# A state-space convolution and an fp8 feed-forward network: sequences sorted by length, gate and up only over those that reach a chunk

## The chip, the cores and the metric

The kernel runs on one core of a Trainium2 chip. The metric is the device time of one execution in microseconds (us), taken as the median of several runs. The engines are TensorE (PE in the profile, its weight loads PEld), VectorE (DVE), ScalarE (ACT), GpSimd (POOL) and SyncE (SP), which issues DMAs. Every engine works through its own instructions in order and waits for the others by semaphores.

## The reference

There are 128 sequences (B) of 32 channels, called heads here (H), and 512 positions (L). Each head is convolved causally with a kernel of its own that a state-space model gives (64 complex modes), plus a skip term D; positions at or past the length of their sequence are set to zero. The result goes through a gated feed-forward network with fp8 rounding before each product, and x is added. Lengths are drawn from 78 to 453.

```python
y = causal_conv(x, K) + x * D[:, None]            # K: 32 heads x 512 taps, from log_dt, C, A
y = y * (arange(512)[None, :] < length[:, None])[:, None, :]
g = fp8(y) @ gate_w.T                             # gate_w, up_w: 1376 x 512
u = fp8(y) @ up_w.T
hidden = silu(g * sg) * (u * su)
out = x + fp8(hidden) @ down_w.T * sd             # down_w: 512 x 1376
```

## The kernel before

Positions lie on the partitions, in four chunks of 128 (LC). The 32 heads are taken in eight groups of four (HG); the columns of a group are its four heads by 128 sequences, T = 512 columns. The weights stay in SBUF from the start, as bf16 views of the f32 that was loaded (every second bf16). The hidden size 1376 is taken in eleven chunks of 128 (IC).

At the start the kernel builds a table of the taps in three batches of heads (`Powers`: 4, 12 and 16 heads), writes it to DRAM, and reads it back as Toeplitz blocks (`toeplitz`, tile `st`). Meanwhile `keep_busy` issues matmuls on zeros (tile `still`). The tables of the later batches are made between other work; those of the last batch on VectorE behind the residual adds of groups 0 and 1 (`between`).

A convolution (`convolve` for heads 0 to 15, `convolve8` for 16 to 31) multiplies f32 Toeplitz blocks, the stationary operand, with chunks of x. It uses sums of chunks (`xs`), which an accumulating DMA from GpSimd makes (L111 to L121), and ends in two PSUM tiles, `sp` and `cp`. ScalarE copies `sp` out; VectorE adds it to `cp` and writes fp8 `q` (L566), then sets the masked positions to zero (L576). Two ScalarE sums over `q` at the end of a group look for values that aren't finite (L580).

`gate_up` makes, for each of the eleven chunks, a gate and an up accumulation of four matmuls each (L612: weights stationary, `q` moving, 512 columns). ScalarE applies silu (L620), VectorE multiplies (L621). `quantise` rounds the product to fp8 in batches of one or two chunks: one ScalarE instruction (L594) and three VectorE instructions (L597 to L599). `Down` multiplies the result `hq` with the down weights (L654: weights stationary, `hq` moving) in four units, one for each chunk of positions; `put_out` adds x (L667), and SP stores the unit.

The stages of two groups are interleaved: after the last gate and up matmul of group g, TensorE runs convolutions of group g + 1 and the down units of g in turn. The order within an engine comes from a scheduler that follows the program order and the readiness of operands, except where `with after(...)` sets an instruction behind another on the same engine. PSUM holds eight tiles of 512 columns: two each of `gp` (also `sp`), `up`, `dp` and `cp`. A second, exact path (`wide`) runs behind a test at the end if a check has failed.

Of the kernel before, what the change touches and what calls it, by code (L numbers as in the profile page):

```python
# [9 lines left out]
F32 = mybir.dt.float32  # L10
# [47 lines left out]
def ssm_fp8_ffn(  # L58
    ctx: ExitStack,
    tc: tile.TileContext,  # L60
    xT: bass.AP,
    lens: bass.AP,
# [5 lines left out]
    outT: bass.AP,  # L68
# [13 lines left out]

    const = ctx.enter_context(tc.tile_pool(name="const", bufs=1))
# [7 lines left out]

    AT = [0, 2, 1, 3]


    SUMS = [(0, 1), (1, 2), (0, 2)]

    def chunk_of(g, c):
        return xT[AT[c] * P : (AT[c] + 1) * P, g * HG : (g + 1) * HG, :].rearrange("p h b -> p (h b)")

    def add_chunks(xg, n):  # L100
        xs = xp.tile([P, len(SUMS), T], F32, name="xs", bufs=1)
        for s, (c0, c1) in enumerate(SUMS[:n]):
            nc.vector.tensor_add(xs[:, s, :], xg[:, AT[c0], :], xg[:, AT[c1], :])
        return xs

    def load_sums(g, n):

        xs = xp.tile([P, len(SUMS), T], F32, name="xs", bufs=1)
        x0, x1, x2 = (chunk_of(g, c) for c in range(3))
        if n == 1:  # L110
            nc.gpsimd.dma_start(xs[:, 0, :], x1)  # L111
            nc.gpsimd.dma_start(xs[:, 0, :], x0, accum_op=ALU.add)
            return xs

        def twice(x):
            return x.unsqueeze(1).to_broadcast([P, 2, T])

        nc.gpsimd.dma_start(xs[:, 0:2, :], twice(x1))  # L118
        nc.gpsimd.dma_start(xs[:, 2, :], x0)
        nc.gpsimd.dma_start(xs[:, 0, :], x0, accum_op=ALU.add)  # L120
        nc.gpsimd.dma_start(xs[:, 1:3, :], twice(x2), accum_op=ALU.add)  # L121
        return xs

    def load_x(g):
        xg = xp.tile([P, LC, T], F32, name="xg")
        nc.sync.dma_start(
            xg.rearrange("p c (h b) -> p c h b", b=B),
            xT[:, g * HG : (g + 1) * HG, :].rearrange("(c p) h b -> p c h b", p=P),
        )
        return xg  # L130
# [3 lines left out]
    len_i = const.tile([P, B], I32, name="len_i")  # L134
    nc.sync.dma_start(len_i, lens.to_broadcast([P, B]))
# [30 lines left out]
    EIGHT = len(batches) - 1  # L166

    RB, RZ = 2 * P // NB, P // NB  # L170
    NRS = [(3 if n == EIGHT else 2) * RB + NA for n in range(len(batches))]
    KPS = [(NR + RZ) * NB for NR in NRS]
    kpads = [dram.tile([h1 - h0, KPS[n]], F32, name=f"kpad{n}") for n, (h0, h1) in enumerate(batches)]
    kts = [kg.tile([NRS[n] + RZ, h1 - h0, NB], F32, name=f"kt{n}") for n, (h0, h1) in enumerate(batches)]
# [22 lines left out]
    last = kg.tile([1, NRS[0]], F32, name="last")  # L197
    nc.gpsimd.memset(last, 0.0)
    nc.gpsimd.memset(last[:, NRS[0] - 1 :], 1.0)

    last8 = kg.tile([1, NRS[EIGHT]], F32, name="last8")

    gas = [kg.tile([P, w, NR + RZ], F32, name=f"ga{n}") for n, (w, NR) in enumerate(zip((HG, HB), NRS[::2]))]
# [41 lines left out]
    keep_busy(12)  # L245
    keep_busy(10, wim)

    class Powers:
# [67 lines left out]
        def products(self):  # L316
# [9 lines left out]
            NR = NRS[self.n]  # L326
# [8 lines left out]
            sums = pair(0, RB)  # L335
            yield nc.vector.tensor_sub(sums, pair(k0, RB), pair(k0 + RZ, 0))
            if self.n == EIGHT:
                yield nc.vector.tensor_sub(sums, sums, pair(k0 + 2 * RZ, RZ))
                yield nc.vector.scalar_tensor_tensor(
                    ga[:, :, 2 * RB : 3 * RB], ga[:, :, k0 + RB : NR], -1.0, ga[:, :, k0 + RB + RZ :], ALU.mult, ALU.subtract  # L340
                )

        def response(self, behind=None):
            NR = NRS[self.n]
# [3 lines left out]
            done = nc.tensor.matmul(kp[:, :, NB - 1], last8 if self.n == EIGHT else last, sm[0:1, 5, self.hs], start=False, stop=True)  # L348
# [48 lines left out]
    len_f = const.tile([P, B], F32, name="len_f")  # L397
    with after(coeffs_there):
        nc.gpsimd.tensor_copy(len_f, len_i)
        row_i = const.tile([P, LC], I32, name="row_i")  # L400
        nc.gpsimd.iota(row_i, pattern=[[P, LC]], base=P - 1, channel_multiplier=-1)
        row_f = const.tile([P, LC], F32, name="row_f")
        nc.gpsimd.tensor_copy(row_f, row_i)


    def build_mask(m, value, chunks=range(LC)):
        for c in chunks:
            done = nc.gpsimd.tensor_scalar(m[:, AT[c], :], len_f, row_f[:, c : c + 1], value, ALU.is_gt, ALU.mult)
        return done

    mask = const.tile([P, LC, B], U8, name="mask")
    all_bits = const.tile([P, 1], F32, name="all_bits")
    with after(first_done):
        nc.vector.memset(all_bits, 255.0)
    with after(copied):
        xs0 = add_chunks(x0, 1)
    with after(build_mask(mask, all_bits, range(1))):
        if IP > I:
            nc.gpsimd.memset(gw[:, :, I:], 0.0)
            nc.gpsimd.memset(uw[:, :, I:], 0.0)  # L420
            nc.gpsimd.memset(dw[I - FI * P :, FI, :], 0.0)
        done = build_mask(mask, all_bits, range(1, LC))
    with after(done):
        for kt in kts[1:]:
            nc.gpsimd.memset(kt, 0.0)
        nc.gpsimd.memset(gas[1][:, :, NRS[EIGHT] :], 0.0)
        nc.gpsimd.memset(last8, 0.0)
        NR = NRS[EIGHT]
        for row, d in ((2 * RB - RZ - 1, -1.0), (3 * RB - RZ - 1, -1.0), (NR - 1, 1.0)):
            nc.gpsimd.memset(last8[:, row : row + 1], d)  # L430
# [3 lines left out]

    shared = [const.tile([P, LC, B], F32, name=f"shared{n}") for n in range(HG)]
    with after(coeffs_there):
        for t in shared:
            nc.gpsimd.memset(t[:, 0, :], 0.0)
    chk = ctx.enter_context(tc.tile_pool(name="chk", bufs=1))

    def toeplitz(pool, h):

        n = next(n for n, (_, h1) in enumerate(batches) if h < h1)
        own = 3 if n == EIGHT else 2
        st = pool.tile([P, 6, P], F32, name="st")
        kpad, at = kpads[n], kpads[n].offset + (h - batches[n][0]) * KPS[n]
        done = nc.sync.dma_start(st[:, 3:6, :], bass.AP(kpad.tensor, at + (2 * own + 1) * P, [[1, P], [1, 3 * P]]))
        done = nc.sync.dma_start(st[:, 3 - own : 3, :], bass.AP(kpad.tensor, at, [[1, P], [2 * P, own], [1, P]]))
        return st, done

    def convolve8(st, xg, xs, j, scale, pool, before, bufs):

        b = slice(j * B, (j + 1) * B)
        k3, k2, k1, K2, K1, K0 = (st[:, n, :] for n in range(6))
        sp = ps.tile([P, 3, B], F32, name="sp", tag="gp")
        for n, k in enumerate((K2, K0, K1)):  # L460
            nc.tensor.matmul(sp[:, n, :], k, xs[:, n, b], start=True, stop=True)  # L461

        sh = pool.tile([P, 4, B], F32, name="sh", bufs=bufs)
        with after(before) if before else ExitStack():
            copied = nc.scalar.activation(sh[:, 0:3, :], sp, AF.Copy, scale=scale)  # L465
        with after(copied):
            copied = nc.scalar.activation(sh[:, 3, :], sp[:, 0, :], AF.Copy, scale=scale)
        t = shared[j]
        nc.vector.tensor_add(t[:, 1:4, :], sh[:, 0:3, :], sh[:, 1:4, :])
        cp = ps.tile([P, LC, B], F32, name="cp")  # L470
        nc.tensor.matmul(cp[:, 0:4:3, :], K0, xg[:, 0:4:3, b], start=True, stop=False)  # L471
        for c, k, x in ((3, k3, 0), (1, k1, 2), (2, k2, 1)):
            done = nc.tensor.matmul(cp[:, AT[c], :], k, xg[:, AT[x], b], start=c != 3, stop=True)  # L473
        return cp, pairs(t), done, copied

    def convolve(h, st, xg, xs, j, scale, pool, before=None, bufs=2):

        if h >= batches[EIGHT][0]:
            return convolve8(st, xg, xs, j, scale, pool, before, bufs)
        b = slice(j * B, (j + 1) * B)
        k3, k2, K2, K1, K0 = (st[:, n, :] for n in range(1, 6))
        sp = ps.tile([P, B], F32, name="sp", tag="gp")
        nc.tensor.matmul(sp, K2, xs[:, 0, b], start=True, stop=True)  # L487
        t = shared[j]
        with after(before) if before else ExitStack():
            copied = nc.scalar.activation(t[:, 1, :], sp, AF.Copy, scale=scale)  # L490
        cp = ps.tile([P, LC, B], F32, name="cp")
        nc.tensor.matmul(cp, K0, xg[:, :, b], start=True, stop=False)  # L492

        nc.tensor.matmul(cp[:, 2:4, :], K1, xg[:, 0:2, b], start=False, stop=False)  # L494
        nc.tensor.matmul(cp[:, 1, :], k2, xg[:, 2, b], start=False, stop=False)  # L495
        done = nc.tensor.matmul(cp[:, 3, :], k3, xg[:, 0, b], start=False, stop=True)  # L496
        return cp, twice(t[:, 0:2, :]), done, copied

    def pairs(y):

        return y.rearrange("p (k c) b -> p k c b", k=2)

    def twice(t):
        return t.unsqueeze(1).to_broadcast([P, 2, 2, B])
# [414 lines left out]
```

## Time and profile before

| | us |
|---|---|
| median of 3 runs (318.44 to 321.06) | 319.95 |
| the profiled execution | 318.58 |
| its span, first to last instruction | 316.8 |
| TensorE busy | 306.5 |
| VectorE busy | 265.4 |
| ScalarE busy | 182.5 |
| GpSimd busy | 29.6 |

The profiled execution is one run; its span runs from the first to the last instruction, and 1.78 us of its time lie around it. The lines that the prediction shows come from the profile's page and from queries of the same trace. A line of the groups has the program line, the engine, the operation, output and inputs, the shapes and the count; then the busy time in us and the mean ns of one; then the idle time of the engine just before these instructions and what ended it. A line of the windows has the stretch, its length, and the busy us of PE, PEld, DVE, ACT and POOL with their counts, the granted TensorE clock, the DMA share and GB/s. A line of the timeline or the chain begins with start and duration. A line of the waits says who waited for whom, how long in all, how often, and the longest. In the DMA lines the last figure is the median time from issue to landing.

### The profile page before, as it was taken

The numbers are of one execution on the slowest core, as the hardware profiler recorded it, in microseconds if no ns is written. First come the engines' busy times: TensorE is split into PE (matmuls) and PEld (weight loads), VectorE is DVE, ScalarE is ACT, GpSimd is POOL, SyncE is SP. The second block draws the span as 40 slices with busy tenths as digits, with TensorE's granted clock in tenths as the row PEclk, the third lists the DMA queues.
The fourth block names the chain that finished last, engine by engine and source line by source line (L and its number), as shares of the span: only waits on it lengthen the run. The fifth ranks groups of instructions, "written<-read, shape, count | busy, mean of one in ns | idle before, by whom it ended". The sixth has DMA issues, their size and how long they took to land.

```text
span 316.8 us, 4622 instructions
## 1 busy us (share of the span) xinstructions
PE 306.5 (97%) x1575; PEld 164.5 (52%) x1575; DVE 265.4 (84%) x477; ACT 182.5 (58%) x372; POOL 29.6 (9%) x72
## 2 busy tenths in 40 slices
PE   8899799999999999999999999999999999999992
PEld 2465346544555446644476446744476446744441
DVE  5985899789988899648998599958998599968992
ACT  5836568557683568446674477546664477266600
POOL 5621000010001000120001200120001200000000
PEclk9999999999999999999999999999999999999998
DMA  3599999562038500599036961389035830020004
GB/s 106 182 284 383 354 360 305 158 160 106 7 85 240 170 1 2 118 302 255 2 99 156 239 170 31 107 282 220 29 99 136 242 55 2 3 98 2 1 33 143
DMA packets 33922, 45.34 MB, mean 143 GB/s; under 512 B 3651, under 2 KB 20035, under 8 KB 33891
## 3 DMA queue, kind: packets, MB, share of 16 engines
q1 hardware_dynamic: 29603, 34.61, 34.8%
q0 software_dynamic: 3232, 7.87, 11.8%
q10 hardware_dynamic: 1056, 2.49, 2.1%
q8 instruction: 14, 0.23, 0.3%
q14 instruction: 17, 0.14, 0.1%
HBM read 36.41 MB, written 8.55 MB: 142 GB/s over the span
## 4 chain that ended last, share of the span: by engine, by line
PE 88%; DMA 5%; DVE 3%; ACT 1%; issue 1%; POOL 0%; DVEq 0%; POOLq 0%; ACTq 0%
PE dp L654 24%; PE up L612 22%; PE gp L612 22%; PE cp L492 4%; DMA uw<-upT 4%; PE sp L461 3%; PE cp L473 3%; PE cp L471 2%; PE cp L494 2%; PE sp L487 1%; PE cp L496 1%; PE cp L495 1%; DMA sm<-ssm 1%; PE kp L347 1%; ACT L208 0%
## 5 line engine op out<-in xcount | busy, mean ns | idle before, releaser
L612 PE MATMUL up<-q,uw 128*128 128x512 fp8e4 x352 | 90.3, 379 | 2.1 <-DMA uw<-upT 2.1
L612 PE MATMUL gp<-q,gw 128*128 128x512 fp8e4 x352 | 90.3, 379 | 0.2 <-DVE q L576 0.2
L620 ACT ACTIVATE s<-gp,psc 128x512 f32<-128x512 f32 x88 | 59.9, 682 | 51.0 <-PE gp L612 50.8
L654 PE MATMUL dp<-hq,dw 128*128 128x512 bf16 (+1 forms) x363 | 79.8, 373 | 0.0
L621 DVE SCALAR_TENSOR_TENSOR v<-up,psc,s 128x512 f32<-128x512 f32 x88 | 65.9, 748 | 14.8 <-PE up L612 11.7
L597 DVE SCALAR_TENSOR_TENSOR v<-m,v 128x1024 f32<-128x1024 bf16 (+1 forms) x56 | 55.8, 996 | 6.3 <-ACT m L594 5.4
L594 ACT ACTIVATE m<-v 128x1024 bf16<-128x1024 f32 (+1 forms) x56 | 48.8, 871 | 17.8 <-DVE v L621 17.3
L612 PEld LDWEIGHTS <-uw 128*128 128x128 bf16 x352 | 34.3, 98 | 44.2 <-DMA uw<-upT 3.0
L612 PEld LDWEIGHTS <-gw 128*128 128x128 bf16 x352 | 34.3, 98 | 41.6 <-DVE q L576 0.3
L598 DVE SCALAR_TENSOR_TENSOR hq<-m,v 128x1024 bf16<-128x1024 bf16 (+1 forms) x56 | 55.6, 993 | 0.1
L654 PEld LDWEIGHTS <-dw 128*128 128x128 bf16 x363 | 35.5, 98 | 36.0
L667 DVE SCALAR_TENSOR_TENSOR xg<-dp,nsc,xg 128x512 f32<-128x512 f32 (+1 forms) x33 | 24.0, 731 | 11.7 <-PE dp L654 11.4
L566 DVE SCALAR_TENSOR_TENSOR q<-cp,inv,shared 128x512 fp8e4<-128x512 f32 x32 | 23.9, 748 | 8.2 <-PE cp L496 8.2
L580 ACT ACTIVATE s<-q 128x1024 bf16<-128x1024 fp8e4 x16 | 16.8, 1048 | 18.3 <-DVE q L576 18.3
L599 DVE TENSOR_SCALAR hq<-hq 128x1024 bf16<-128x1024 bf16 (+1 forms) x56 | 20.6, 367 | 0.2
L465 ACT ACTIVATE sh<-sp,inv 128x384 f32<-128x384 f32 x16 | 9.2, 572 | 15.9 <-PE sp L461 15.9
L492 PE MATMUL cp<-xg,st 128*128 128x512 f32 x32 | 16.4, 594 | 0.0
L243 PE MATMUL nothing<-still 128*128 128x512 bf16 x48 | 13.5, 442 | 1.4 <-POOL still L180 1.4
L461 PEld LDWEIGHTS sp<-xs,st 128*128 128x128 f32 x96 | 12.9, 192 | 1.7
L473 PEld LDWEIGHTS cp<-xg,st 128*128 128x128 f32 x96 | 13.2, 191 | 0.8
L118 POOL DMA_DIRECT2D xs<-xT x4 | 3.0, 753 | 112.0 <-PE sp L461 79.1
L461 PE MATMUL sp<-xs,st 128*128 128x128 f32 x96 | 13.3, 275 | 0.0
(145 smaller groups left out, 241.4 us busy)
## 6 DMA issues: line engine op xcount, KB each, us to landing
st<-kpad SPq DMA_DIRECT2D x48, 192.0 KB, 4.1
xg<-xT SPq DMA_DIRECT2D x8, 1024.0 KB, 8.8
outT<-xg SPq DMA_DIRECT2D x31, 256.0 KB, 4.0
xs<-xT POOLq DMA_DIRECT2D x8, 512.0 KB, 7.9
xs<-xT POOLq DMA_DIRECT2D x14, 256.0 KB, 5.5
dw<-downT SPq DMA_DIRECT2D x1, 2560.0 KB, 13.8
st<-kpad SPq DMA_DIRECT2D x16, 128.0 KB, 4.8
gw<-gateT SPq DMA_DIRECT2D x2, 768.0 KB, 8.9
```

The costliest lines, as they stand in the source:

```text
L461: nc.tensor.matmul(sp[:, n, :], k, xs[:, n, b], start=True, stop=True)
L473: done = nc.tensor.matmul(cp[:, AT[c], :], k, xg[:, AT[x], b], start=c != 3, stop=True)
L492: nc.tensor.matmul(cp, K0, xg[:, :, b], start=True, stop=False)
L566: nc.vector.scalar_tensor_tensor(pairs(q[:, :, j * B : (j + 1) * B]), pairs(cp), inv[:, 0:1], t, ALU.mult, ALU.add, saturate=False,)
L594: done = nc.scalar.activation(m[:, 0:F], v, AF.Abs, scale=2.0**20 * (1.0 + 2.0**-6), accum_out=acc)
L597: nc.vector.scalar_tensor_tensor(v, m[:, 0:F], 1.5 * 2.0**14, v, ALU.max, ALU.add)
L598: nc.vector.scalar_tensor_tensor(out, m[:, 0:F], 1.5 * 2.0**14, v, ALU.max, ALU.subtract)
L612: multiplied = nc.tensor.matmul(o, w[:, c, i * P : (i + 1) * P], q[:, AT[c], :], start=(c == 0), stop=(c == LC - 1),)
L620: nc.scalar.activation(s, gp, AF.Silu, scale=pgate)
L621: product = nc.vector.scalar_tensor_tensor(v[:, (i - i0) * T : (i - i0 + 1) * T], up, pup, s, ALU.mult, ALU.mult)
L654: done = nc.tensor.matmul(self.dps[n], dm[:, i, c * P : (c + 1) * P], self.hq[:, i, t0:t1], start=(i == 0), stop=(i == IC - 1),)
L667: added = nc.vector.scalar_tensor_tensor(o, self.dps[n], ndown, o, ALU.mult, ALU.add)
```

## The change

The sequences are ranked by length on the chip: VectorE counts for each sequence how many are longer (a key of length and number keeps the order strict), and a 128 x 128 permutation in bf16 is made from the ranks. The convolution now has x as the stationary operand and the Toeplitz blocks as the moving one, so `q` comes out with sequences on the partitions. `sort` multiplies each chunk of `q` of a head with the first columns of the permutation, 128, 124, 84 and 40 of them (`CAPS`) for the four chunks; this transposes and sorts at once, and ScalarE copies the result to `qs` in fp8. Gate and up then stream only these columns for each chunk. If more sequences reach a chunk than it has columns, `fits` sends the kernel to the wide path.

All heads use one convolution of 1152 columns; `convolve8`, its further sums and its longer tables are gone. In the down product `hq` is the stationary operand and the weights are the moving one; a unit is now a head, with sequences on the partitions in sorted order. The x that is added is gathered by an indirect DMA from GpSimd (`load_sorted`, 1 MB a group), and the output is scattered by one indirect DMA for each unit, also from GpSimd, instead of a store from SP. The x for the convolution has one buffer instead of three.

The order is written out anew. `gate_up` chains matmuls and VectorE instructions; `STEPS` says how many VectorE steps of the quantise jobs follow each product, nine in all (jobs 0 to 2). The other four jobs come later: job 3 ahead of the first convolution output, job 4 ahead of the third, jobs 5 and 6 behind the fourth. The down units start behind all four convolutions. The checks of `q` come behind the sixth silu of `gate_up`. All loads of gate and up weights are issued from SP. `keep_busy` has two matmuls more at each of two places.

```diff
+    CAPS = [B, 124, 84, 40]
+    OFF = [sum(CAPS[:c]) for c in range(LC)]
+    NQ = sum(CAPS)
+
+    CHUNKS = [3, 1, 2, 0]
...
+    def load_sums(g):
+
+        xs = xp.tile([P, T], F32, name="xs", bufs=1)
+        nc.gpsimd.dma_start(xs, chunk_of(g, 1))
+        return xs, nc.gpsimd.dma_start(xs, chunk_of(g, 0), accum_op=ALU.add)
 
     def load_x(g):
-        xg = xp.tile([P, LC, T], F32, name="xg")
+        xg = xp.tile([P, LC, T], F32, name="xg", bufs=1)
         nc.sync.dma_start(
...
-    keep_busy(12)
-    keep_busy(10, wim)
+    keep_busy(14)
+    keep_busy(12, wim)
...
+        nc.gpsimd.tensor_scalar(lf, len_i, 0.0, float(L), ALU.max, ALU.min)
+        nc.gpsimd.iota(col_i[:, 0:B], pattern=[[-1, B]], base=B - 1, channel_multiplier=0)
+        nc.gpsimd.iota(col_i[:, B:], pattern=[[0, 1]], base=B - 1, channel_multiplier=-1)
+        nc.gpsimd.tensor_copy(col_f, col_i)
+        nc.gpsimd.tensor_scalar(key, lf, float(B), None, ALU.mult)
+        nc.gpsimd.tensor_add(key, key, col_f)
+        for s, c in enumerate(CHUNKS):
+            nc.gpsimd.iota(l_i[:, s * P : (s + 1) * P], pattern=[[-1, P]], base=(c + 1) * P - 1, channel_multiplier=0)
+        mask_there = nc.gpsimd.tensor_scalar(mask, l_i, own, 255.0, ALU.is_lt, ALU.mult)
...
+        xs0 = add_chunks(x0)
+        nc.vector.tensor_scalar(counted, key[:, 0:B], key[:, B:], 0.0, ALU.is_gt, ALU.add, accum_out=rank)
+
+        nc.vector.tensor_scalar(rank, rank, -1.0, B - 1.0, ALU.mult, ALU.add)
+        sorted_there = nc.vector.tensor_scalar(perm, col_f[:, 0:B], rank, None, ALU.is_equal)
...
+    def rows(t, n):
+
+        return t.rearrange("b h l -> (b h l)").rearrange("(r n) -> r n", n=n)
+
+    def at(index, n):
+        return bass.IndirectOffsetOnAxis(ap=index[:, n : n + 1], axis=0)
+
+    def load_sorted(g):
+        xn = xp.tile([P, HG * L], F32, name="xn", bufs=2)
+        nc.gpsimd.indirect_dma_start(xn, None, rows(x, HG * L), at(index_g, g))
+        return xn
...
+        sp = ps.tile([P, P], F32, name="sp", tag="gp")
+        nc.tensor.matmul(sp, xs[:, b], st[:, 1, :], start=True, stop=True)
         t = shared[j]
         with after(before) if before else ExitStack():
-            copied = nc.scalar.activation(t[:, 1, :], sp, AF.Copy, scale=scale)
+            copied = nc.scalar.activation(t[:, 0, :], sp, AF.Copy, scale=scale)
+        cp = ps.tile([P, LC, P], F32, name="cp")
+        nc.tensor.matmul(cp[:, 1:4:2, :], xg[:, 0, b], st[:, 2:4, :], start=True, stop=False)
+        nc.tensor.matmul(cp[:, 0:4:2, :], xg[:, 2, b], st[:, 2:4, :], start=False, stop=False)
+        nc.tensor.matmul(cp[:, 1:3, :], xg[:, 1, b], st[:, 3:5, :], start=False, stop=False)
+        nc.tensor.matmul(cp[:, 0, :], xg[:, 3, b], st[:, 3, :], start=False, stop=False)
+        done = nc.tensor.matmul(cp[:, 0, :], xg[:, 0, b], st[:, 0, :], start=False, stop=True)
+        return cp, t.unsqueeze(1).to_broadcast([P, 2, 2, P]), done, copied
...
+            def sort(q, qs, j, before):
+
+                pq = ps.tile([P, NQ], F32, name="pq", tag="up")
+                for c in range(LC):
+                    done = nc.tensor.matmul(
+                        pq[:, OFF[c] : OFF[c] + CAPS[c]],
+                        q[:, j, CHUNKS.index(c) * P : (CHUNKS.index(c) + 1) * P],
+                        perm[:, 0 : CAPS[c]],
+                        start=True,
+                        stop=True,
                     )
+                with after(before):
+                    return done, nc.scalar.activation(qs[:, j, :], pq, AF.Copy, saturate=False)
...
+            STEPS = {1: 1, 2: 2, 3: 1, 5: 1, 6: 1, 7: 1, 9: 1, IC - 1: 1}
+            EARLY = firsts[3]
...
+                            o = o.rearrange("p (h n) -> p h n", h=HG)
+                            with after(multiplied) if multiplied else ExitStack():
+                                for c in range(LC):
+                                    multiplied = nc.tensor.matmul(
+                                        o[:, :, 0 : CAPS[c]],
+                                        w[:, c, i * P : (i + 1) * P],
+                                        qs[:, :, OFF[c] : OFF[c] + CAPS[c]],
+                                        start=(c == 0),
+                                        stop=(c == LC - 1),
+                                    )
...
+                        if i == i1 - 1:
+                            n = g * NB_Q + b
+                            jobs.append(quantise(hq[:, i0:i1, :].rearrange("p c t -> p (c t)"), v, big[:, n : n + 1]))
+                        with after(done):
+                            for done in itertools.islice(todo, STEPS.get(i, 0)):
+                                pass
+                        if i == 5:
+                            with after(done):
+                                between()
+                            with after(gated):
+                                check_q(g, q)
...
                             self.dps[n],
-                            dm[:, i, c * P : (c + 1) * P],
-                            self.hq[:, i, t0:t1],
+                            self.hq[:, i, j * B : (j + 1) * B],
+                            dm[:, i, l0:l1],
...
+                    where = at(index, self.g * HG + j) if l1 - l0 == L else at(index_2, l0 // (l1 - l0))
+                    nc.gpsimd.indirect_dma_start(rows(out, l1 - l0), where, o, None)
...
+                else:
+                    with after(convolved):
+                        done, sines_there = sort(q, qs, j - 1, sines_there)
...
+                last, sent = multiplied, None
+                for j in range(HG):
+                    if j in (0, 2):
+                        with after(done):
+                            *_, done = jobs.pop(0)
+                    with after(last), after(done):
+                        last, done, loaded, sent = conv(g + 1, q, j, xg, xs, sent)
+                    if j >= 2:
+                        with after(last):
+                            last, sent = sort(q, qs, j - 2, sent)
+                with after(loaded):
+                    if g == 0:
                         load_down()
+                    if g + 2 < G:
+                        x_next = load_x(g + 2)
+                if g + 2 < G:
+                    xs_next, summed = load_sums(g + 2)
+                with after(summed):
+                    xn_next = load_sorted(g + 1)
+                with after(sent):
                     if g == 0:
+                        sent = others[1].magnitudes()
                     else:
                         list(itertools.islice(lows, 4))
+                for n in range(2):
+                    with after(last):
+                        last = d.multiply(n, 0, LATE)
+                    with after(last):
+                        last, sent = sort(q, qs, 2 + n, sent)
+                for job in jobs:
+                    with after(done):
+                        *_, done = job
+                with after(last):
+                    last = d.multiply(2, 0, LATE)
+                for n in range(HG):
+                    if (g, n) == (G - 2, HG - 1):
+                        break
+                    with after(last):
+                        last = d.multiply(n, LATE if n < 3 else 0, IC)
+                    with after(done):
+                        done = d.put_out(n)
...
+            for job in jobs:
                 with after(done):
+                    *_, done = job
+            with after(done):
+                done = before.put_out(HG - 1)
+            for i0, i1 in ((0, EARLY), (EARLY, LATE)):
+                for n in range(3):
+                    with after(last):
+                        last = d.multiply(n, i0, i1)
+            for n in range(len(halves)):
+                with after(last):
+                    last = d.multiply(n, LATE if n < 3 else 0, IC)
```

## The prediction

> **What bounds the kernel now.** I read the busy line and the chain first, then the windows cut at the first gate matmul of each group of four heads, then the groups by form, the waits, and the timelines of start and end.
>
> ```profile
> PE 306.5 (97%) x1575; PEld 164.5 (52%) x1575; DVE 265.4 (84%) x477; ACT 182.5 (58%) x372; POOL 29.6 (9%) x72
> PE 88%; DMA 5%; DVE 3%; ACT 1%; issue 1%; POOL 0%; DVEq 0%; POOLq 0%; ACTq 0%
> ...
> 25.85:64.86 39.01, 36.94 (x173) 18.83 (x174) 32.17 (x50) 25.53 (x56) 2.31 (x3) 1.00 0.92 306
> 139.22:174.99 35.77, 35.77 (x190) 20.12 (x188) 30.75 (x48) 21.54 (x45) 3.17 (x4) 1.00 0.55 152
> 279.92:316.80 36.88, 31.12 (x157) 14.85 (x154) 27.65 (x46) 14.67 (x27) 0.00 (x0) 0.96 0.15 53
> ```
>
> In a middle group TensorE is busy for all of 35.77 us (second number), at full clock (1.00), and VectorE (fourth) for 30.75. Only 5 us lie between the bound and the next engine: a change that takes more than that from TensorE gains no more than VectorE allows.
>
> ```profile
> 64.86 0.86 PE gp L612 x4
> ...
> L621 DVE SCALAR_TENSOR_TENSOR v<-up,psc,s 128x512 f32<-128x512 f32 x88 | 65.9, 748 | 14.8 <-PE up L612 11.7 <-PE gp L612 2.3 <-ACT s L620 0.9
> L597 DVE SCALAR_TENSOR_TENSOR v<-m,v 128x1024 f32<-128x1024 bf16 x32 | 39.2, 1224 | 2.3 <-ACT m L594 1.4
> L598 DVE SCALAR_TENSOR_TENSOR hq<-m,v 128x1024 bf16<-128x1024 bf16 x32 | 39.0, 1219 | 0.0
> L654 PEld LDWEIGHTS <-dw 128*128 128x128 bf16 x363 | 35.5, 98 | 36.0
> L580 ACT ACTIVATE s<-q 128x1024 bf16<-128x1024 fp8e4 x16 | 16.8, 1048 | 18.3 <-DVE q L576 18.3
> L469 DVE TENSOR_TENSOR shared<-sh 128x384 f32<-128x384 f32 x16 | 8.9, 556 | 0.0
> PE up L612 <- DMA uw<-upT: 2.1, 2, 1.9
> 49.33 0.39 PE L487 MATMUL sp<-xs,st 128*128 128x128 f32 x2
> 51.29 4.05 PE L654 MATMUL dp<-hq,dw 128*128 128x512 bf16 x18
> 30.60 0.89 POOL L112 DMA_DIRECT2D xs<-xT  x1 [6.63 <-DMA xs<-xT]
> 177.94 1.27 POOL L121 DMA_DIRECT2D xs<-xT  x1
> xs<-xT POOLq DMA_DIRECT2D x14, 256.0 KB, 5.5
> outT<-xg SPq DMA_DIRECT2D x31, 256.0 KB, 4.0
> 311.08 0.48 DVE L667 SCALAR_TENSOR_TENSOR xg<-dp,nsc,xg 128x256 f32<-128x256 f32 x1 [0.89 <-PE dp L654]
> ```
>
> The first line is the chain's: four matmuls of 512 columns in 0.863 us, 0.2158 each, 0.4215 ns a column. One convolution of 1152 columns takes 51.29 - 49.33 = 1.96 us.
>
> **TensorE, part by part.** (a) Gate and up: each accumulation streams 4 x (128 + 124 + 84 + 40) = 1504 columns instead of 2048. At 0.4215 ns that is 0.634 us for 0.863; 22 of them are 14.0 us for 19.0, so 5.0 us less a group. (b) Convolution: every head takes the 1152 columns of the plain form, 1.95 us, 7.8 a group. The three-sum form of heads 16 to 31 takes 1.82 in the trace (7.3), so groups 4 to 7 lose 0.5. (c) Sorting: 16 small matmuls a group, 376 columns a head. The columns alone are 0.16 us a head; four matmuls each with its weight load, at the f32 convolution's pace (six in 0.66 us, L473), are 0.44. The bf16 load (98 ns) is half the f32 one (191 ns), so I take 0.20, nearer the columns: 0.8 a group. (d) Down: the same 44 matmuls, 9.5 us. The weights become the moving operand, read at every second bf16, which no row shows: at best 0.2158, at worst 0.43, a record of 512 f32 columns, also read four bytes apart. I take 0.2158: loading the same strided dw as weights costs 98 ns, no more than loading the dense "still" (109). Sum 14.0 + 7.8 + 0.8 + 9.5 = 32.1 us.
>
> The Trainium skill, "TensorE: Matmul & The Clock Gate", section "Back-to-back issue gap", speaks against (a) and (c): it gives some 81 ns for a matmul of 128 columns in a stream of loads and matmuls. By it sorting would be an estimated 0.32 us a head and the 160-column matmul 0.081 for 0.067, some 6 us more over the kernel.
>
> **VectorE and ScalarE.** VectorE keeps 11 products, 7 quantise jobs, 4 convolution outputs with mask and 4 residual adds a group; it loses only the L469 adds (2.2 us in groups 4 to 7). In a row an instruction takes its duration less 0.085 us (a product each 0.66), but one that reads its predecessor's result starts 0.04 after its end, and the jobs now run step after step: 2.9 us for two chunks. Sum: products 7.3, jobs 15.9, outputs 4.0, adds 2.7: 29.9. ScalarE loses a copy or two a head and gains one of 376 columns (0.56, by L465); its two checks of q (2 x 1.14 us with the read of the sum) move from the down stage to behind the sixth silu.
>
> **A group, walked through by hand** (offsets from its first gate matmul; a matmul's result reaches the next engine 0.26 us after its slot, as from L612 to L620). Gate and up want 14.0 us. The checks hold ScalarE from 7.8 to 10.1, silu 6 comes late, and chunks 6 to 8 wait 0.9 us for PSUM; the last waits 0.2 for a product: end at 15.1. VectorE, with nine quantise steps laid between the products, has done them at 17.7. It then must run job 3 before the first convolution output: 20.5, outputs at 21.3 and 22.3, job 4 to 25.4, outputs to 27.4, jobs 5 and 6 to 30.7. TensorE has two convolutions done at 19.0 and the third's sum at 19.2, but its main part needs the PSUM of the first: it starts at 21.3, a wait of 2.1. Four convolutions and two sorts end at 25.4; three down units of nine chunks and two sorts (6.2) at 31.6; their last chunks and the fourth unit (3.7) at 35.3. TensorE waits 3.2 us of these; VectorE idles 1.7 before the adds, 1.3 before the last and the rest in small pieces. Of the 5 us taken out, 0.8 goes to sorting, 0.5 to convolution, 3.2 to waits for VectorE and ScalarE: 35.3 for 35.77.
>
> Group 1 takes 36.4 and group 2 36.7: the last batch's tables are made on VectorE as fillers (5.6 us behind group 1's adds) and their 1.34 us of matmuls follow. Group 6 lacks its last unit: 32.9. The seven sum to 247.3, before 254.07 (25.85 to 279.92); group 0 alone had 39.0, with its waits for weights.
>
> **Start.** The key, sort order and mask go to POOL and VectorE. POOL is free from 8 to 19.7, where the mask is needed; 512 columns are four L408 rows (0.95 each), and with the small operations it ends near 15. Were it later, each us would delay the first gate. The three VectorE operations (0.75) fit into 0.95 idle before 18.8. Four more warming matmuls push the first response by 0.2. Two sorts among the convolutions add 0.4, and the last output has to be sorted and copied: 1.05. First gate at 27.5 for 25.85. The weights of chunks 6 to 10 go from ACT's queue to SP's, ahead of the next x: by the bytes moved (7.6 MB by 31.7 us) they have landed near 34, needed at 35.6; the waits on uw go.
>
> **DMA.** SP loses 33 stores and gains one load of lengths. POOL gains 8 gathers of 1 MB and 33 scatters, loses 6 sum loads. x has one buffer now, but some 27 us for a load of 8.8. On POOL the gather and four scatters queue behind the accumulating load, which waits 4 to 7 us; nobody needs them for a group. Only the end is exposed. No indirect issue is in the trace; plain ones take 0.57 to 1.27 us. I take 0.9 (L112), and allow 2.5, twice the largest, above.
>
> The Trainium skill, "SBUF — State Buffer", section "SBUF: two separate sides", warns of this: descriptors written by GpSimd stand still while VectorE holds the shared port. If that is so here, the POOL queue's landing has it inside; no figure of the page goes into the sum.
>
> **Sum.** 27.5 + 247.3 = 274.8 for the last group's gate. There gate and up take 15.1 and the held unit 2.4; down then waits for jobs 3 to 6, done at 26.8: TensorE ends after 30.6, at 305.4 (before 311.06), the first whole add at 303.0, the last at 306.1. Five scatters 0.9 apart: the last issues at 306.6. It lands 4.7 later (3.2 of a half unit on SP, plus 5.5 - 4.0), and 2.0 follow, as before (316.8 - 311.56 - 3.2). Span 313.3; with the 1.78 us around it 315.1 against 318.58 for the profiled execution, 1.1% less. The runs' median is 319.95: 316.
>
> **Rivals.** *VectorE keeps up*: its 29.9 us fit into 32.1. Against: its order is written out, job 3 ahead of the first output. Without 3.2 us of waits in seven groups and 2 at the end: 292.
> *Short matmuls cost a weight load each* (slower). At 0.11 us, sorting is 0.44 a head and the 160-column matmul 0.11 for 0.067: a group becomes 37.2, the end 12.2 later: 328. For: f32 loads pace the convolution. Against: the bf16 load is half as long. From 0.08 us a load on the gain is used up.
> *Down at half pace* (slower): at 0.43 a group takes 44.7: 387. Against: the dw load row.
> *POOL late*: issues of 2.5 us put the last scatter at 313.0 instead of 306.6: 322.
> *It doesn't do what it says*: lengths that break the caps would run the wide branch over everything, far slower; the drawn lengths leave 120, 77 and 21 sequences against 124, 84 and 40, so it gets no chance.
>
> **How the numbers follow.** The forecast 0.50 (own range 307 to 324), VectorE keeps up 0.14, weight loads 0.17, half pace 0.05, POOL 0.14. One per cent, about what a measurement of this kernel can tell from no change, is 316.8 to 323.1. Faster 0.30 + 0.14 + 0.03 = 0.47; within 0.17 + 0.03 + 0.06 = 0.26; slower 0.03 + 0.14 + 0.05 + 0.05 = 0.27. The range 300 to 330 leaves out half pace and most of the first rival.
>
> **What would show it.** Right: 22 accumulations of 0.63 us a group; TensorE waiting about 2 us for VectorE's output in each third convolution; middle windows near 35.3. Wrong: sorting over 0.3 us a head; down rows off 0.2158; middle windows of 32 to 33, or 36.5 and more; a span that ends 10 us after the last add.

## The result, and the profile after

The changed kernel takes 336.42 us (median of four runs, 333.06 to 340.11), the kernel before 319.24 (318.44 to 321.06). The ratio is 1.046, with a 95% interval of 1.038 to 1.054: 4.6% slower, where 1% faster was forecast, and above the range of 300 to 330. The four runs lie in two pairs, near 333 and near 340 us; the ratio is of the lower pair and a fifth run of 335.75, the profile is of a run at 340.11 (span 338.0), and so the sums below are made for both.

The page of the changed kernel: busy times, the chain, the group of the scatters; then the windows of group 0, a middle group and the last one (columns as before: window, length, PE, PEld, DVE, ACT, POOL, clock, DMA share, GB/s).

```profile
PE 289.0 (86%) x1708; PEld 172.9 (51%) x1708; DVE 264.8 (78%) x464; ACT 182.5 (54%) x388; POOL 71.8 (21%) x122
PE 53%; DVE 15%; DMA 12%; ACT 9%; issue 6%; SPq 1%; POOL 0%; POOLq 0%; ACTq 0%; DVEq 0%
...
L706 POOL DMA_INDIRECT out<-xn,index x33 | 36.1, 1093 | 136.7 <-DVE xn L702 58.6
```

```profile
28.00:72.28 44.28, 35.48 (x197) 20.94 (x196) 30.42 (x46) 24.83 (x56) 7.48 (x11) 0.92 0.93 298
181.59:217.00 35.41, 33.50 (x198) 20.34 (x197) 29.80 (x44) 20.43 (x45) 6.53 (x7) 1.00 0.47 143
285.33:338.00 52.67, 27.71 (x157) 14.20 (x155) 28.75 (x49) 15.06 (x29) 9.31 (x9) 0.83 0.11 42
```

TensorE lost 17.5 us of work (306.5 to 289.0), as it was meant to. Its place in the chain fell from 88% to 53%; DMA's rose from 5% to 12%. The middle window is right where it was forecast, 35.41 for 35.3. The first and the last window are not: group 0 takes 44.28 us for 39.01 before, and the last one 52.67 for 36.88, although it holds 3.4 us less of TensorE's work.

The end of the last group: VectorE's last residual add, then GpSimd's issues (start, length, what ended the wait ahead of it), and the line of the waits that sums them up.

```profile
315.54 0.48 DVE L702 SCALAR_TENSOR_TENSOR xn<-dp,nsc,xn 128x256 f32<-128x256 f32 x1
```

```profile
312.59 0.97 POOL L706 DMA_INDIRECT out<-xn,index  x1 [18.50 <-DVE xn L702]
316.05 0.97 POOL L706 DMA_INDIRECT out<-xn,index  x1 [2.50 <-DVE xn L702]
321.23 0.97 POOL L706 DMA_INDIRECT out<-xn,index  x1 [4.21 <-DMA out<-xn,index]
325.02 0.97 POOL L706 DMA_INDIRECT out<-xn,index  x1 [2.82 <-DMA out<-xn,index]
328.48 0.97 POOL L706 DMA_INDIRECT out<-xn,index  x1 [2.49 <-DMA out<-xn,index]
331.62 0.97 POOL L706 DMA_INDIRECT out<-xn,index  x1 [2.17 <-DMA out<-xn,index]
```

```profile
POOL out L706 <- DMA out<-xn,index: 37.8, 13, 4.4
```

An issue takes 0.97 us, near the 0.9 that was assumed. But each scatter waits for the landing of the one before it, and so they stand 3.1 to 5.2 us apart. (The second's wait is put down to VectorE. In run 9 below it starts 1.28 us behind the first instead of 3.46, so here too it was the landing.) The last is issued 15.6 us after the last add, and the span ends 22.0 us after it; before it was 5.2.

Group 0: SyncE's issues of the second kpad (the taps of a batch of heads, written to DRAM), of the first st (the Toeplitz blocks) that reads it and of dw (the down weights); then TensorE's wait for uw (the up weights) and its first down product.

```profile
27.66 0.32 SPq L330 DMA_DIRECT2D kpad<-kt  x1
...
38.94 0.34 SPq L478 DMA_DIRECT2D st<-kpad  x1
...
44.19 0.82 SPq L138 DMA_DIRECT2D dw<-downT  x1
```

```profile
38.51 0.81 PE L648 MATMUL up<-qs,uw 128*128 128x512 fp8e4 x4 [2.07 <-DMA uw<-upT]
...
60.10 4.00 PE L689 MATMUL dp<-dw,hq 128*128 128x512 bf16 x9 [5.26 <-DMA dw<-downT]
```

The write of kpad, 54 KB, lands 11.3 us after its issue, behind the weights of chunks 6 to 10 that the change put ahead of it on this queue; dw is issued behind it and TensorE waits 5.26 us for it. The nine products after the wait take 4.0 us instead of 2.0. In the window of these products the granted clock, third from the end, is 0.50:

```profile
60.10:63.89 3.79, 3.79 (x9) 1.29 (x9) 0.00 (x0) 1.79 (x4) 1.97 (x2) 0.50 1.00 276
```

### The profile page after: what moved, and what is told of

Its sections match the earlier page's. It is cut to its first block, busy times and chain, and to the rows that moved or that the text cites. A ratio compares the mean times of both kernels' runs of the same rounds, so it can differ in the third digit from the quotient of the medians.

```text
span 338.0 us, 4890 instructions
## 1 busy us (share of the span) xinstructions
PE 289.0 (86%) x1708; PEld 172.9 (51%) x1708; DVE 264.8 (78%) x464; ACT 182.5 (54%) x388; POOL 71.8 (21%) x122
## 4 chain that ended last, share of the span: by engine, by line
PE 53%; DVE 15%; DMA 12%; ACT 9%; issue 6%; SPq 1%; POOL 0%; POOLq 0%; ACTq 0%; DVEq 0%
PE dp L689 22%; PE gp L648 9%; PE up L648 8%; DVE hq L626 5%; DMA dw<-downT 5%; ACT s L656 5%; DMA out<-xn,index 4%; DMA kpad<-kt 3%; DVE v L625 3%; DVE v L658 3%; PE cp L498 3%; PE cp L499 2%; PE cp L500 2%; ACT s L610 2%; ACT m L624 2%
## 5 line engine op out<-in xcount | busy, mean ns | idle before, releaser
L689 PE MATMUL dp<-dw,hq 128*128 128x512 bf16 (+1 forms) x363 | 85.2, 386 | 7.6 <-DMA dw<-downT 5.3
L648 PE MATMUL up<-qs,uw 128*128 128x512 fp8e4 (+1 forms) x352 | 70.3, 321 | 4.8 <-DVE v L658 2.3
L648 PE MATMUL gp<-qs,gw 128*128 128x512 fp8e4 (+1 forms) x352 | 70.3, 321 | 1.2 <-ACT s L656 0.7
L706 POOL DMA_INDIRECT out<-xn,index x33 | 36.1, 1093 | 136.7 <-DVE xn L702 58.6
L689 PEld LDWEIGHTS <-hq 128*128 128x128 bf16 x363 | 33.6, 97 | 48.6 <-issue 7.3
L648 PEld LDWEIGHTS <-gw 128*128 128x128 bf16 x352 | 32.1, 97 | 27.8 <-issue 1.9
L702 DVE SCALAR_TENSOR_TENSOR xn<-dp,nsc,xn 128x512 f32<-128x512 f32 (+1 forms) x33 | 23.0, 728 | 26.3 <-PE dp L689 26.1
L604 ACT ACTIVATE qs<-pq 128x376 fp8e4<-128x376 f32 x32 | 15.2, 480 | 49.9 <-PE pq L596 49.9
L498 PE MATMUL cp<-st,xg 128*128 128x256 f32 x64 | 19.8, 392 | 9.9 <-DVE q L579 9.9
L499 PE MATMUL cp<-st,xg 128*128 128x256 f32 x64 | 19.0, 379 | 0.0
L500 PE MATMUL cp<-st,xg 128*128 128x256 f32 x64 | 19.0, 379 | 0.0
L496 ACT ACTIVATE shared<-sp,inv 128x128 f32<-128x128 f32 x32 | 11.7, 365 | 12.1 <-PE sp L493 12.1
```

Source lines behind the costliest of these rows:

```text
L498: nc.tensor.matmul(cp[:, 1:4:2, :], xg[:, 0, b], st[:, 2:4, :], start=True, stop=False)
L499: nc.tensor.matmul(cp[:, 0:4:2, :], xg[:, 2, b], st[:, 2:4, :], start=False, stop=False)
L500: nc.tensor.matmul(cp[:, 1:3, :], xg[:, 1, b], st[:, 3:5, :], start=False, stop=False)
L648: multiplied = nc.tensor.matmul(o[:, :, 0 : CAPS[c]], w[:, c, i * P : (i + 1) * P], qs[:, :, OFF[c] : OFF[c] + CAPS[c]], start=(c == 0), s ...
L689: done = nc.tensor.matmul(self.dps[n], self.hq[:, i, j * B : (j + 1) * B], dm[:, i, l0:l1], start=(i == 0), stop=(i == IC - 1),)
L706: nc.gpsimd.indirect_dma_start(rows(out, l1 - l0), where, o, None)
```

## Experiments

**Theory A**: the scatters wait for each other's landing because all write one tensor, and that sets the end. **Rivals**: B, the price is GpSimd's issues; C, the groups' bodies got longer. For group 0, **theory D**: the order on SyncE's queue makes dw late; **E**: the DMA engines are full there whatever the order. For the body, **theories F to K** on where the 5 us of columns a group went. Ratios are to the kernel before, run on the same chip, with 95% intervals; times are medians.

**1. Plain stores.**

```diff
-                    nc.gpsimd.indirect_dma_start(rows(out, l1 - l0), where, o, None)
+                    nc.sync.dma_start(out[:, self.g * HG + j, l0:l1], o)
```

> All 33 scatters to out become plain stores from SP, in sorted order (the un-sorting of the rows is left out). Theory A, each scatter to out waits for the landing of the one before it, and after the last add that is 22 us where the kernel before had 5.2: without the chain the end comes about 5 us after the last add, 15 to 17 us less than the changed kernel, a ratio to before near 1.00. Theory B, the price is the issue on GpSimd, 0.97 us each, six of them at the end: 5 to 6 us less, ratio near 1.03. Theory C, the body of the groups is what got longer: at most 2 us less, ratio 1.04 or more.

324.99 us, ratio 1.020 [1.015, 1.024]. The last add ended at 315.5 and the span at 323.6, 8.1 us later: 14 us of the 22 were the scatters'. The total is worse than theory A's 1.00; group 0 still took 43.6 us in the profiled run. By its last group the run speaks for A: B would leave 16 us after the last add. The middle groups took 35.41 us, as in the changed kernel and less than the 35.77 before: of theory C only group 0 is left.

**2. One scatter a group**, `rows(out, HG * L), at(index_g, self.g)` for the whole xn, after the fourth add.

> One scatter of 1 MB for each group, after its fourth head's add, in place of four or five of 128 to 256 KB; 8 in place of 33. Theory A (landings in a row): after the last add one issue of 1.0 us, a landing of 5 to 8 us (the gathers of the same size took 8.3 us beside other transfers) and 2 us, so 8 to 11 us in place of 22: 11 to 14 us less than the changed kernel, ratio near 1.01. Theory B (issues): four issues fewer at the end, 4 us less, ratio near 1.03. Theory C (body): no change, or worse by the landing of the large scatter, ratio 1.04 or more.

Ratio 1.011 [1.006, 1.015], of the four lowest runs (up to 324.58) of ten from 319.8 to 327.2; the profiled one, 327.19, had 44.2 us in group 0. The span ended 9.6 us after the last add: inside A's 8 to 11, not B's 18.

**3 and 4. Group 0's queues.** In 3 the weights of chunks 6 to 10 go back to ScalarE's queue; in 4 only the write of the second kpad goes there:

```diff
-            written = nc.sync.dma_start(kpads[self.n].rearrange("h (a b) -> a h b", b=NB), kt)
+            queue = nc.scalar if self.n == 1 else nc.sync
+            written = queue.dma_start(kpads[self.n].rearrange("h (a b) -> a h b", b=NB), kt)
```

> The loads of the gate and up weights of chunks 6 to 10 go back to ScalarE's queue, where the kernel before had them, so the write of kpad and the loads behind it don't stand behind them on SP's. Theory D, the order on SP's queue makes dw late in group 0 (dw issued at 44.2 us, landed at 60.1, TensorE idle for 5.3 us and then at half clock for 4 us): dw is issued near 36 to 38 and lands near 52 to 55, group 0 gets shorter by 5 to 9 us, ratio to before 1.02 to 1.03. Theory E, the DMA engines are full from 25 to 62 us with 2 MB of gathers more than before, and the order doesn't matter: 0 to 2 us less, ratio 1.04 or more.

> Only the write of the second batch's kpad (72 KB) goes to ScalarE's queue; all weights stay on SP's. Theory D (order on SP's queue): the write lands 3 us after its issue at 28 us instead of at 38.9, the loads of st and dw are issued some 6 to 8 us earlier, group 0 is shorter by 4 to 8 us, ratio 1.02 to 1.03. Theory E (DMA engines full whatever the order): 0 to 2 us less, ratio 1.04 or more.

(The write is 54 KB, not 72.) Ratios 1.052 [1.045, 1.058] and 1.047 [1.043, 1.050], as the changed kernel's: by the totals theory E. The traces tell more. Run 4, ScalarE's issue, then SyncE's and TensorE's lines as above:

```profile
27.76 0.58 ACTq L331 DMA_DIRECT2D kpad<-kt  x1
```

```profile
35.73 0.34 SPq L479 DMA_DIRECT2D st<-kpad  x1
...
41.18 0.40 SPq L138 DMA_DIRECT2D dw<-downT  x1
```

```profile
55.32 2.19 PE L690 MATMUL dp<-dw,hq 128*128 128x512 bf16 x8 [0.80 <-DMA dw<-downT]
```

```profile
28.08:65.61 37.53, 33.23 (x195) 20.28 (x197) 30.42 (x46) 24.50 (x56) 7.48 (x11) 1.00 1.04 344
278.65:331.60 52.95, 27.67 (x156) 14.20 (x155) 28.75 (x49) 15.04 (x29) 9.07 (x9) 0.83 0.11 42
```

dw is issued 3.0 us earlier, its wait falls to 0.8, the clock stays full, and group 0 takes 37.5 us: 6.8 less than in the profile of the changed kernel, where D expected 4 to 8. In run 3 it takes 38.6, 5.7 less where 5 to 9 were expected; there dw isn't waited for, and uw is for 3.5 us. Yet the four runs of 4, 333.5 to 333.9, only equal the changed kernel's lower pair, and run 3's (333.9 to 337.4) are no better.

All runs together say more than these two. In the four profiles with the write behind the weights on SyncE's queue (the changed kernel, 1, 2, 5) the first st that reads it is issued at 38.4 to 38.9 us and dw at 44.1 to 45.3, and group 0 takes 42.6 to 44.3. In the eight others it is 35.7 to 36.2 and 40.8 to 41.7, and group 0 takes 36.6 to 39.1. The seven kernels with the write on ScalarE's queue (4 and 6 to 11, 40 runs) vary by 1.7 us at most, each within itself; the changed kernel varies by 7 us, run 2 by 7.4. So D holds for what is lost in the runs near 340. The edit gains nothing on those near 333, and no profile of the unaltered kernel near 333 says what they look like.

The write moved up less than expected (it took 8.0 us to land, not 3). The Trainium skill, "DMA: Bandwidth & Descriptors", section "Issuing engines are not separate DMA queues", says that another issuing engine saves only the time of the issue, since all share 16 engines. Here a write moved past 2.4 MB of weights landed 3.2 us earlier, with a DMA share of 0.9 to 1.0 in both: more than an issue's time (0.3 to 0.6 us). In run 3 it stayed on SyncE's queue with these weights gone from it, and took 8.2 us: what stands ahead of it on its queue counted here, not the engine that issues it.

**5. The changed kernel again**, for a profile near 333 us.

> The changed kernel once more, unaltered, for a profile of a run near 333 us beside the one of 340. Theory D': what parts the two is the 5 us wait for dw and the half clock behind it, so here group 0 takes 37 to 38.5 us in place of 44.4, the last add ends near 309, and the 22 us after it stay. Rival: group 0 takes 44 us here too and the 7 us are missing in the middle groups or after the last add.

339.3 and 339.6 us, group 0 at 42.6. dw is late again (first product at 58.82), but TensorE's wait for it is 2.3 us here; another 2.0 us go on a late st ahead of it, and the clock is granted at 0.61 in the nine products behind the wait. What a run at 333 looks like it can't tell, and I take run 4 for it, which has the same time; that is assumed, not shown.

**6. One scatter in the last group only**, with 4's edit:

```diff
+                    if self.g < G - 1:
                         nc.gpsimd.indirect_dma_start(rows(out, l1 - l0), where, o, None)
+                    elif n == len(self.units) - 1:
+                        nc.gpsimd.indirect_dma_start(rows(out, HG * L), at(index_g, self.g), self.xn, None)
```

> Only the last group's five scatters become one of 1 MB after the last add (the other groups keep one for each head), and the write of the second kpad is on ScalarE's queue as in the run before. Theory A (each scatter waits for the landing of the one before): the scatter of group 6's fourth head, 256 KB, has landed by the last add, so the end comes 1.0 + 4.7 + 2 = 7.7 us after it in place of 22.3, and the time is 333.7 - 14.6 = 319, ratio to before 1.00. Theory B (issues alone): 4 us less, 329.5, ratio 1.035.

320.70 us, ratio 1.004 [1.001, 1.007]: 13.0 us less than run 4 by one edit in one group. The last add ends at 309.15, the scatter is issued at once, and the span ends 9.7 us after the add (7.7 expected): it lands 6.5 us after its issue starts (5.7 expected), and 3.0 follow (2).

```profile
305.71 0.97 POOL L708 DMA_INDIRECT out<-xn,index  x1 [18.73 <-DVE xn L703]
309.43 0.97 POOL L710 DMA_INDIRECT out<-xn,index_g  x1 [2.75 <-DVE any_bad L566]
```

**7. The check of q moved** from behind the sixth silu to the end of the group, on top of 6:

```diff
-                            with after(gated):
-                                check_q(g, q)
+                            if g == 0:
+                                with after(gated):
+                                    check_q(g, q)
...
+                with after(sent):
+                    sent = check_q(g + 1, q)
```

> As the run beside it, and ScalarE's check of q (two passes of 1.24 us) goes from the middle of the gate and up products, where a silu stands behind it, to the end of the group, where ScalarE is idle for 6 us. Theory F, TensorE and VectorE wait for that silu: 0.5 to 0.9 us less for each of groups 1 to 6 and the last, 4 to 6 us in all, 314, ratio near 0.985. Theory G, VectorE's sum of work sets the period: no more than 1 us in all, ratio 1.00.

315.89 us, ratio 0.991 [0.987, 0.994]; the middle groups go from 35.41 to 34.64. That is 4.8 us less than run 6, within F's 4 to 6: theory F.

**8. No column saved**: 6 with `CAPS = [B, B, B, B]`.

> As e6, with all four chunks' gate and up over all 128 sequences (2048 columns in place of 1504): the sorting stays and saves no column. Theory H, the columns saved reach the period: TensorE's 22 accumulations go from 0.637 to 0.86 us, 4.9 us a group, of which the third convolution's wait of 1.7 us and smaller ones take up part: the middle groups go from 35.4 to 38.2 to 39, the time to 319 + 21 to 25 = 340 to 344, ratio near 1.07. Theory G, VectorE sets the period: at most 36.5 us a group, 327 or less, ratio 1.025 or less.

345.68 us, ratio 1.084 [1.080, 1.088]. Theory H, and a little more than it: a middle group takes 39.05 us where 38.2 to 39 were expected. The windows of a middle group, here, in 7 and in 10 below:

```profile
185.13:224.18 39.05, 38.02 (x197) 21.14 (x196) 30.13 (x44) 21.32 (x45) 6.71 (x7) 1.00 0.40 121
```

```profile
173.24:207.88 34.64, 33.17 (x197) 20.29 (x196) 29.75 (x44) 20.72 (x45) 6.52 (x7) 1.00 0.44 141
```

```profile
169.87:203.12 33.25, 33.02 (x195) 20.06 (x196) 29.75 (x44) 20.74 (x45) 7.08 (x7) 1.00 0.49 144
```

TensorE's busy time (second number) falls by 4.5 us from 8 to the changed kernel's 33.50, its group by 3.64: the saved columns do reach the period. The change pays them out again: without them its group takes 3.3 us more than the 35.77 before, with sorting, a slower down product and waits in it.

**9. The last group's scatters to five tensors of their own** (4's edit; the last group's rows of out are left out):

```diff
+                    to = rows(out, l1 - l0)
+                    if self.g == G - 1:
+                        to = dram.tile([B * H * L // (l1 - l0), l1 - l0], F32, name=f"scratch{n}")
-                    nc.gpsimd.indirect_dma_start(rows(out, l1 - l0), where, o, None)
+                    nc.gpsimd.indirect_dma_start(to, where, o, None)
```

> As the run with only kpad's write on ScalarE's queue (333.7 us), but the last group's five scatters go to five tensors of their own in DRAM, so no two write the same tensor; the last group's rows of out are left out. Theory A, the wait is for an order of writes to one tensor: the scatters are issued as soon as their adds are done, 1 us apart or as the adds come, the last one at about 309.6, and the end is 1.0 + 2.7 + 2 us behind it: 5.5 to 7 us after the last add in place of 22.3, 318 us, ratio 1.00. Theory B', GpSimd or its queue takes one scatter at a time, wherever it goes: spacing stays at 3.4 us, 331 to 334, ratio 1.045.

320.59 us, ratio 1.004 [1.000, 1.007].

```profile
305.21 0.97 POOL L710 DMA_INDIRECT out<-xn,index  x1 [18.72 <-DVE xn L703]
306.48 0.97 POOL L710 DMA_INDIRECT scratch<-xn,index  x1 [0.30 <-DVE xn L703]
307.76 0.97 POOL L710 DMA_INDIRECT scratch<-xn,index  x1 [0.30 <-DVE xn L703]
309.04 0.97 POOL L710 DMA_INDIRECT scratch<-xn,index  x1 [0.30 <-DVE any_bad L566]
310.31 0.97 POOL L710 DMA_INDIRECT scratch<-xn,index  x1 [0.30 <-issue]
311.59 0.97 POOL L710 DMA_INDIRECT scratch<-xn,index  x1 [0.30 <-issue]
```

Same instruction, same queue, same bytes, other tensors: the scatters stand 1.28 us apart in place of 3.1 to 5.7 in run 4. So the wait is the program's own, for the order of writes to `out`, and B' is ruled out. Why the program has it is read from the kernel and not tested apart: the rows are known only on the chip, and each scatter names the whole of `out` as its target. Theory A was 2 to 4 us too low for the end (9.4 us after the last add, not 5.5 to 7): the 1.28 add up over five, which puts the last issue at 311.6 instead of 309.6, and 6.4 us follow it instead of 5.7.

**10. VectorE's order**, on top of 7: the outputs of the first two convolutions go ahead of all but one instruction of the two quantise jobs; two sorts go behind the second down product.

```diff
-                    if j in (0, 2):
-                        with after(done):
-                            *_, done = jobs.pop(0)
                     with after(last), after(done):
                         last, done, loaded, sent = conv(g + 1, q, j, xg, xs, sent)
+                    if j == 0:
+                        with after(done):
+                            done = next(jobs[0])
+                    if j == 1:
+                        for _ in range(2):
+                            with after(done):
+                                *_, done = jobs.pop(0)
...
                     with after(last):
                         last = d.multiply(n, 0, LATE)
+                for n in range(2):
                     with after(last):
                         last, sent = sort(q, qs, 2 + n, sent)
```

> As the run with the check moved (315.9 us), and VectorE takes the outputs of the first two convolutions ahead of all but one instruction of the two quantisations that stood before them, and the sorts of heads 2 and 3 come after the down products of heads 0 and 1. Theory I, the third convolution's wait of 1.4 us is one of order: it goes, the middle groups go from 34.65 to 33.2 to 33.6 us, 8 us less in all, 306 to 309, ratio 0.965. Theory G, VectorE's sum sets the period: the wait reappears at the first down product, groups at 34.3 or more, 313 to 316, ratio 0.985 to 0.99.

308.66 us, ratio 0.966 [0.959, 0.972]: faster than both kernels, with the edits of 4, 6, 7 and this one together. The window above shows why: 33.25 us, of which TensorE is busy for 33.02 with the same VectorE time of 29.75. Theory I; the wait was one of order.

**11. Down with a dense moving operand**: 7 with `dm = dw.bitcast(BF16)[:, :, 0:L]`, other values than the weights.

> As the run with the check moved (315.9 us), but down multiplies by the first 512 of dw's 1024 16-bit values in a row, next to each other, in place of every second one (other values than the weights). Theory J, the step of two in the moving operand makes 0.2262 of 0.2158 us: down falls to 0.216 each, 0.46 us less a group, 3.3 us in all with the tail's, 312.5, ratio 0.98. Theory K, it is the weight load of a new operand for each: no change, 0.226, ratio 0.99.

313.07 us, ratio 0.980 [0.974, 0.987], 2.8 us less than run 7. Nine products, with the sort behind them, here and in 7:

```profile
231.80 2.10 PE L692 MATMUL dp<-dw,hq 128*128 128x512 bf16 x9
233.74 0.33 PE L598 MATMUL pq<-perm,q 128*128 128x128 bf16 x4
```

```profile
199.80 2.19 PE L691 MATMUL dp<-dw,hq 128*128 128x512 bf16 x9
201.84 0.33 PE L597 MATMUL pq<-perm,q 128*128 128x128 bf16 x4
```

From the start of the nine to the start of the sort it is 1.94 / 9 = 0.2156 us against 2.04 / 9 = 0.227: theory J, the step of two costs 5%. A middle group falls from 34.64 to 34.21 us:

```profile
205.31:239.52 34.21, 32.62 (x195) 20.36 (x196) 29.75 (x44) 20.12 (x43) 7.04 (x7) 1.00 0.46 139
```

## Why the prediction was wrong

Set against run 4, the last add comes at 309.3 where 306.1 was forecast, and the span ends 22.3 us after it instead of 7.2: of the 18.3 us missing in the span (331.6 for 313.3), **15.1 are behind the last add and 3.2 ahead of it**. In the profiled run of 340 it is 14.8 and 9.9.

- *The step that failed: "Five scatters 0.9 apart: the last issues at 306.6."* The issue was sized well (0.97). From the last issue to the end 6.7 was forecast and 6.4 measured, which is luck: the scatter of a half unit lands 2.4 us after its issue, not 4.7, and 4.0 us follow instead of 2.0. What was left out is the wait between them: five scatters that name one tensor are issued one landing apart, 3.1 to 5.2 us, so the last issues 15.6 us after the last add instead of 0.5. "Only the end is exposed" was right: the 13 waits sum to 37.8 us, and those of the middle groups cost nothing: run 1, without them, has the same 35.41 us. The rival *POOL late* had the place, with 6.4 us more, but the wrong mechanism: it made each issue longer (2.5 us).
- *"The waits on uw go"* failed. The last weights of chunks 6 to 10, those of up, land at 38.5, not near 34, and TensorE waits 2.1 us for them; the text then said nothing of what stands behind them on that queue: kpad, st, dw. That is the second miss: group 0 takes 44.3 us in the profile for 35.3. In run 4 it takes 37.5, with 1.7 us of waiting for uw and 0.8 for dw in it.
- *Start*: first gate at 28.0 for 27.5. *Groups 1 and 2*: 37.6 and 36.3 for 36.4 and 36.7.
- *The walk through a middle group* held, in its parts too: 35.41 for 35.3. Accumulations take 0.637 us for 0.634; in group 6 gate and up end after 14.9 us for 15.1, the third convolution's main part starts at 20.9 for 21.3, and it waits 1.67 us for VectorE's output for 2.1. Run 10 shows that this wait was one of order, not of VectorE's sum; *VectorE keeps up* is what it becomes with another order.
- *Sorting*: 0.18 us a head for 0.20. The Trainium skill's 81 ns for a matmul of 128 columns ("TensorE: Matmul & The Clock Gate", "Back-to-back issue gap") would make an estimated 0.32: four matmuls with their loads, 94 columns on average, take 44 ns each here. *Short matmuls cost a weight load each* falls with it.
- *Down*: mis-sized by 5%: 0.226 for 0.2158, 0.43 us a group (run 11), which the shorter wait of the convolution made good. *Half pace* falls.

Of the 5.0 us a group taken off TensorE in gate and up, the groups kept 0.4. Run 7 gives back 0.8 by moving a check off a silu's way, run 10 another 1.4 by VectorE's order: the change had room for 2.2 us a group more.

Not settled: why the same program takes 333 us in some runs and 340 in others. All its profiles are of runs near 340, with dw late; that dw comes in time near 333, and that the order of arrival decides (the DMA share is 0.93 to 1.04 of all engines in group 0), is argued, not shown. The end of the last group also stays longer than before: 9.7 us follow the last add with one scatter (run 6), 8.1 with plain stores (run 1), 5.2 in the kernel before.

## What to carry over

Before stores are turned into scatters with an index from the chip, write down what each of them must wait for: here scatters into one tensor stood in a row, a landing apart, and the last group has nothing to hide that behind. Give the last group one scatter. And when a load is moved to another queue, list what it now stands ahead of, and who waits for that.

## What the runs showed of the hardware

In the changed kernel the issue of an indirect scatter took 0.97 to 1.8 us (median 0.99), that of a gather of 1 MB 0.97 to 1.1. Successive scatters to separate tensors stood 1.28 us apart (run 9). At the end of the changed kernel a scatter of 256 KB landed 2.7 to 4.4 us after its issue began, one of 128 KB after 2.4; one of 1 MB landed after 4.5 to 5.2 us in run 2 and after 6.1 to 6.5 in runs 6, 7, 8, 10 and 11. A bf16 moving operand with a step of two elements cost 5% (0.227 us for 0.2156 with 512 columns, runs 7 and 11). Behind 5.3 us without matmuls TensorE's clock was granted at 0.50 for 3.8 us of products; behind a wait of 0.8 us (run 4) it stayed at 1.00.
